# Seven-product scores, masks made ahead in layer 0, and early rows beside the signs: one change of a graph-attention kernel

## Chip, cores, metric

One core of one Trainium2 chip. The time is that of the device in microseconds (us), the median of several executions. One row of work is 128 nodes. "Before" and "after" are the two kernels. "Layer 0" is the stage between the signs and the hidden products. In the profile PE is TensorE (the matmuls), PEld its weight loads, DVE VectorE, ACT ScalarE, POOL GpSimd and SP SyncE. BF16, F32 and F32R are number formats; a product of 512 columns costs 0.227 us in F32R and 0.86 us in F32 (worked out in the prediction). "In order" means that an engine does not pass by an operation that has to wait.

## The reference

N = 4096 nodes, D = 512 features, `adj` is 4096 x 4096 in float32 and sparse.

```python
# layer 0
xw = max(sign(x), 0) @ sign(w0).T
x1 = layernorm(x + relu(adj @ xw))
# layer 1
node_att = softmax(x1 @ node_w, axis=0)
h = x1 @ edge_w
e = where(adj > 0, h @ h.T, NEG_BIG)          # the scores
edge_att = softmax(e, axis=1)
out = layernorm(x1 + (adj * (node_att * edge_att)) @ (x1 @ w1) + bias)
```

## The kernel before

It has five stages: signs, aggregation of layer 0 (32 rows), hidden products, scores, and aggregation of layer 1. A row of layer 0 reads its 128 x 4096 strip of `adj` as two transposed 1 MB halves (`at`), splits each quarter into `hi` (ScalarE) and `lo` (VectorE), and multiplies both by `xw` in F32R:

```python
# start: signs in BF16, 16 products a group of 512 nodes
nc.sync.dma_start(xt, x_t[:, ts(g, W)]...)
nc.vector.tensor_scalar(ba, xt, 0.0, None, ALU.is_gt)
...
def aggregate(b):                                # a row of layer 0
    ...
    for half in range(2):
        nc.sync.dma_start(at, adj_t[b, :, ts(half, HB), :])
        for q in range(2):
            nc.scalar.copy(hi, aq)
            nc.vector.tensor_sub(lo, aq, hi.bitcast(F32))
            for c in range(QC):
                nc.tensor.matmul(acc, hi[:, c, :], xw[:, kb, :], ...)
                nc.tensor.matmul(acc, lo[:, c, :], xw[:, kb, :], ...)
    ...                                          # VectorE: relu, layer norm
    nc.vector.tensor_tensor_reduce(scr, ...)
    nc.gpsimd.tensor_add(scr, xb, bias_b)
    nc.gpsimd.dma_start(x1_d[ts(b, P), :], scr)  # GpSimd also stores the row's other parts
```

The scores (products `pe`) are made for pairs of groups of 512 nodes, with four F32 products of K = 128 for each 128 x 512 block. VectorE makes the mask of each block there, from `adj` in F32.

## Time and profile before

2028.7 us (2028.4 to 2031.6, 4 runs). The stages below are read from the first and last start of a line's matmuls.

| Stage of before | us |
|---|---|
| start to the third row's first product (37.3 + two rows of 14.93) | 67.2 |
| from there to the first hidden product (layer 0) | 450.9 |
| hidden products | 96.4 |
| scores, to the first product of the last stage | 514.7 |
| last stage | 896.3 |

Two of the page's groups list the line, engine and operation, what it writes and reads with its shapes, then the busy time, the mean ns of one, and the idle time of the engine before it with its releaser. The third line is a transfer: its issuing queue, count, size and median us to landing.

```profile
L209 PE MATMUL acc<-xw,lo 128*128 128x512 f32 x1024 | 399.4, 390 | 0.6 <-DVE lo L205 0.5
...
L205 DVE TENSOR_TENSOR lo<-at,hi 128x1024 fp32r<-128x1024 f32 x128 | 168.7, 1318 | 147.1 <-ACT hi L203 147.1
...
at<-in_adj_t_dram SPq DMA_DIRECT2D x64, 1024.0 KB, 5.1
```

PE waited 0.6 us for `lo` in 1024 products. VectorE itself idled 147 us before `lo`, so it has slack on average.

### The profile page before, as it was taken

The numbers are of one execution on the slowest core, as the hardware profiler recorded it, in microseconds if no ns is written. First come the engines' busy times: TensorE is split into PE (matmuls) and PEld (weight loads), VectorE is DVE, ScalarE is ACT, GpSimd is POOL, SyncE is SP. The second block draws the span as 40 slices with busy tenths as digits, with TensorE's granted clock in tenths as the row PEclk, the third lists the DMA queues.
The fourth block names the chain that finished last, engine by engine and source line by source line (L and its number), as shares of the span: only waits on it lengthen the run. The fifth ranks groups of instructions, "written<-read, shape, count | busy, mean of one in ns | idle before, by whom it ended". The sixth has DMA issues, their size and how long they took to land.

```text
span 2025.5 us, 17689 instructions
## 1 busy us (share of the span) xinstructions
PE 2004.4 (99%) x6268; PEld 1108.3 (55%) x6268; DVE 1243.5 (61%) x1759; ACT 691.5 (34%) x1195; POOL 401.5 (20%) x485
## 2 busy tenths in 40 slices
PE   9999999999999999999999999999999999999997
PEld 4888888888544454545555444444444444444443
DVE  3555555556534554445545897786759775977634
ACT  4333333333113666666666521131221220222100
POOL 0243333334300000000001111140124111321101
PEclk9999999999999999999999999999999999999999
DMA  9566566565009786867767887765666765685421
GB/s 328 186 220 203 196 216 210 201 209 173 29 0 351 260 302 229 308 231 272 280 257 265 330 329 258 250 248 198 249 237 251 260 246 201 227 283 201 172 70 62
DMA packets 118153, 455.73 MB, mean 225 GB/s; under 512 B 10288, under 2 KB 10288, under 8 KB 93488
## 3 DMA queue, kind: packets, MB, share of 16 engines
q0 software_dynamic: 48128, 241.20, 31.6%
q1 hardware_dynamic: 69360, 212.36, 31.6%
q8 instruction: 49, 0.80, 0.2%
q10 hardware_dynamic: 576, 1.05, 0.1%
q14 instruction: 40, 0.33, 0.0%
HBM read 355.99 MB, written 98.57 MB: 224 GB/s over the span
## 4 chain that ended last, share of the span: by engine, by line
PE 96%; DMA 3%; DVE 1%; ACT 0%; issue 0%; SPq 0%; ACTq 0%; POOLq 0%; POOL 0%; DVEq 0%
PE ps L479 38%; PE pe L356 21%; PE acc L209 11%; PE acc L208 11%; PE po L531 5%; PE seven L89 5%; PE pt L377 3%; DMA a<-in_adj_dram 2%; PE pw L181 1%; PE pt L238 1%; DMA xt<-in_x_t_dram 1%; DVE lo L205 0%; PE ptm L405 0%; DMA xb<-x_d 0%; ACT a L342 0%
## 5 line engine op out<-in xcount | busy, mean ns | idle before, releaser
L356 PE MATMUL pe<-hT 128*128 128x512 f32 (+3 forms) x1152 | 475.5, 557 | 0.0
L479 PE MATMUL ps<-q,lop 128*128 128x512 f32 x1024 | 446.9, 592 | 0.0
L208 PE MATMUL acc<-xw,hi 128*128 128x512 f32 x1024 | 401.6, 392 | 0.0
L209 PE MATMUL acc<-xw,lo 128*128 128x512 f32 x1024 | 399.4, 390 | 0.6 <-DVE lo L205 0.5
L479 PE MATMUL ps<-t,lop 128*128 128x512 f32 x768 | 332.9, 592 | 0.0
L479 PEld LDWEIGHTS ps<-q,lop 128*128 128x128 f32 x1024 | 193.9, 190 | 240.8 <-issue 237.0
L356 PEld LDWEIGHTS pe<-hT 128*128 128x128 f32 x1152 | 205.0, 191 | 184.0 <-issue 174.8
L434 ACT ACTIVATE q<-q 128x2048 f32<-128x2048 f32 x64 | 122.3, 1911 | 407.8 <-DVE q L431 394.2
L205 DVE TENSOR_TENSOR lo<-at,hi 128x1024 fp32r<-128x1024 f32 x128 | 168.7, 1318 | 147.1 <-ACT hi L203 147.1
L479 PEld LDWEIGHTS ps<-t,lop 128*128 128x128 f32 x768 | 145.9, 190 | 183.7 <-issue 180.3
L440 DVE SCALAR_TENSOR_TENSOR q<-ac,q 128x512 f32<-128x512 f32 x256 | 198.9, 830 | 53.6 <-ACT q L434 39.1
L203 ACT CAST hi<-at 128x1024 fp32r<-128x1024 f32 x128 | 134.6, 1052 | 272.6 <-PE acc L208 271.3
L209 PEld LDWEIGHTS acc<-xw,lo 128*128 128x128 f32 x1024 | 192.3, 188 | 41.0 <-DVE lo L205 1.7
L208 PEld LDWEIGHTS acc<-xw,hi 128*128 128x128 f32 x1024 | 192.3, 188 | 39.3
L338 DVE CUSTOM_DVE_ANT_0 a<-a,pe 128x512 f32<-128x512 f32 x112 | 76.7, 687 | 206.9 <-ACT s L363 206.9
L342 ACT ACTIVATE a<-a,nmax_c 128x512 f32<-128x512 f32 x256 | 183.5, 718 | 45.8 <-DVE nmax_c L338 45.5
L483 DVE TENSOR_TENSOR over<-over,ps 128x512 f32<-128x512 f32 x168 | 113.6, 681 | 107.8 <-PE ps L479 107.7
L431 DVE CUSTOM_DVE_ANT_1 q<-q,mrow 128x2048 f32<-128x2048 f32 x64 | 148.5, 2325 | 40.3 <-DMA q<-s_d 36.2
L363 ACT COPY s<-pe 128x512 f32<-128x512 f32 (+2 forms) x144 | 77.7, 543 | 138.4 <-PE pe L356 120.3
L531 PE MATMUL po<-over 128*128 128x512 f32 x256 | 115.9, 600 | 3.7 <-DVE xb L540 3.7
L425 POOL DMA_DIRECT2D ac<-in_adj_t_dram x64 | 48.8, 763 | 325.3 <-DVE q L440 253.4
L377 PEld LDWEIGHTS pt<-ident,s 128*128 128x128 f32 x496 | 62.1, 141 | 68.7 <-issue 57.7
(107 smaller groups left out, 1553.8 us busy)
## 6 DMA issues: line engine op xcount, KB each, us to landing
at<-in_adj_t_dram SPq DMA_DIRECT2D x64, 1024.0 KB, 5.1
ac<-in_adj_t_dram POOLq DMA_DIRECT2D x64, 1024.0 KB, 6.7
a<-in_adj_dram SPq DMA_DIRECT2D x64, 1024.0 KB, 7.5
q<-s_d POOLq DMA_DIRECT2D x64, 1024.0 KB, 7.8
lop<-lop_d SPq DMA_DIRECT2D x112, 512.0 KB, 4.1
s_d<-s POOLq DMA_DIRECT2D x36, 1024.0 KB, 4.8
s_d<-t POOLq DMA_DIRECT2D x28, 1024.0 KB, 6.2
xb<-in_x_dram SPq DMA_DIRECT2D x32, 256.0 KB, 3.1
```

The lines of the kernel that those rows point to most:

```text
L203: nc.scalar.copy(hi, aq)
L205: nc.vector.tensor_sub(lo, aq, hi.bitcast(F32))
L208: nc.tensor.matmul(acc, hi[:, c, :], xw[:, kb, :], start=(kb == 0), stop=False)
L209: nc.tensor.matmul(acc, lo[:, c, :], xw[:, kb, :], start=False, stop=(kb == NB - 1))
L342: lambda: nc.scalar.activation(e, e, AF.Exp, bias=nmax_c[:, b, c : c + 1], scale=-1.0, accum_out=sum_c[:, b, c : c + 1])
L356: nc.tensor.matmul(pe[:, lo * P :], hT[:, k, ts(A * BG + i, P)], hT[:, k, (B * BG + lo) * P : (B + 1) * W], start=(k == 0), stop=(k == KD ...
L377: nc.tensor.transpose(pt[:, j, :], s[:, i, ts(j, P)], ident)
L431: nc.vector._custom_dve(TENSOR_ADD_SAT, out=q, in0=q, in1=mrow.unsqueeze(1).to_broadcast([P, BG, W]), s0=0.0, s1=-HUGE)
L434: nc.scalar.activation(q, q, AF.Exp)
L440: nc.vector.scalar_tensor_tensor(qc, a[:, :, c, :], 0.0, qc, ALU.max, ALU.mult)
L479: nc.tensor.matmul(ps, lop[:, c, ts(h, P)], rop[m][:, c, :], start=(c == 0), stop=(c == BG - 1))
L531: nc.tensor.matmul(po, (lower if k // 2 else upper)[:, k % 2, ts(i, P)], w1_s[:, k, :], start=(k == 0), stop=(k == KD - 1),)
```

## The change

It has four parts:

1. **Scores.** The blocks of two pairs of groups are multiplied together in seven products instead of eight.
2. **Masks.** Most masks are made in layer 0, in 80 pieces: a piece of `adj` is loaded (512 KB), turned into a BF16 mask in place by VectorE, and stored (256 KB). The scores load that.
3. **Light pairs last.** The cheap score pairs come at the end, beside the first loads of the last stage.
4. **Signs.** Two rows of signs ride in one F32R product. Rows 0 and 16 of layer 0 are aggregated beside the signs.

The core of the diff, with cuts and in another order:

```diff
+        pieces = deque((r, j, c) for r in range(NG) for j in range(BG) for c in range(0, r + 1, 2))
+        pair = wp.tile([P, 2, 2 * W], F32, name="pair", tag="we_s")
+        single = wp.tile([P, 2 * W], F32, name="single", tag="quarter", bufs=2)
+        bufs = deque([pair[:, 0, :], pair[:, 1, :], single])
+        def premask():
+            if loaded and (len(loaded) == 2 or not pieces):
+                (r, j, c), a = loaded.popleft()
+                m = a.bitcast(BF16).rearrange("p (c w) -> p c w", c=2)[:, :, :W]
+                nc.vector.tensor_scalar(m, a.rearrange(...), 0.0, NEG_BIG, ALU.is_le, ALU.mult)
+                nc.gpsimd.dma_start(mask_d[r][:, c : c + 2, j, :], m)
+                bufs.append(a)
+            if pieces:
+                r, j, c = pieces.popleft()
+                a = bufs.popleft()
+                nc.gpsimd.dma_start(a, adj[ts(r * BG + j, P), c * W : (c + 2) * W])
+                loaded.append(((r, j, c), a))
         def aggregate(b):
...
-            for half in range(2):
+            for half in range(0 if b in early else 2):
...
                     nc.vector.tensor_sub(lo, aq, hi.bitcast(F32))
+                    if (half, q) != (0, 0):
+                        premask()
...
+        early = [0, HB]
+        def halves(g):                       # slices of the two early rows
+            for n, b in enumerate(early):
+                nc.sync.dma_start(a, adj_t[b, :, ts(g, BG), :])
+                nc.scalar.copy(hi[:, ts(n, BG), :], a)
+                nc.vector.tensor_sub(lo[:, ts(n, BG), :], a, ...)
...
-                nc.vector.tensor_scalar(ba, xt, 0.0, None, ALU.is_gt)
+                nc.vector.tensor_scalar(over, xt[:, :, W // 2 :], 0.0, TWO, ALU.is_gt, ALU.mult)
+                nc.vector.scalar_tensor_tensor(ba, xt[:, :, : W // 2], 0.0, over, ALU.is_gt, ALU.add)
...
+    class Couple:                            # two pairs of groups, seven products
+        def quad(self, q, between):
+            multiply(y, 0, True); nc.scalar.copy(c11, y)
+            multiply(x, 1, True); nc.vector.tensor_add(c11, c11, x)
+            multiply(y, 5); nc.scalar.copy(c12, y)
+            ...
```

## The prediction

> **What bounds the kernel now.** I read the page from the top: busy time per engine, the slices, the chain that ended last; then PE's waits, the busy time of each engine by stretch, and PE's timeline for the pitch of its matmuls.
>
> From the page of the kernel before:
>
> ```profile
> PE 2004.4 (99%) x6268; PEld 1108.3 (55%) x6268; DVE 1243.5 (61%) x1759; ACT 691.5 (34%) x1195; POOL 401.5 (20%) x485
> ...
> PE 96%; DMA 3%; DVE 1%; ACT 0%; issue 0%; SPq 0%; ACTq 0%; POOLq 0%; POOL 0%; DVEq 0%
> ```
>
> PE is busy for 2004.4 of 2025.5 us and is 96% of the chain, so the time is the sum of PE's work plus 21 us of gaps. Whatever removes PE work shortens the kernel, unless a new wait comes in.
>
> Its busy time by stretch (window; length, PE, PEld, DVE, ACT, POOL busy; clock, DMA share, GB/s): the start, layer 0, the scores, the aggregation.
>
> ```profile
> 5.00:35.00 30.00, 27.17 (x121) 11.71 (x120) 13.66 (x19) 16.11 (x28) 0.00 (x0) 1.00 1.04 391
> 200.00:400.00 200.00, 200.00 (x911) 165.51 (x910) 113.14 (x147) 66.34 (x80) 68.79 (x76) 1.00 0.63 206
> 614.00:1129.00 515.00, 510.55 (x1652) 262.60 (x1651) 260.44 (x614) 328.96 (x783) 39.40 (x72) 1.00 0.76 278
> 1129.00:1984.00 855.00, 855.00 (x2018) 380.10 (x2018) 634.36 (x680) 169.88 (x163) 164.71 (x191) 1.00 0.65 233
> ```
>
> The start is limited by the transfers (391 GB/s, share 1.04); the rest by PE, with room on the others.
>
> A matmul's "mean ns" is its latency, so its price must come from start to start in the timeline (start, duration, what):
>
> ```profile
> 1082.66 3.60 PE L356 MATMUL pe<-hT 128*128 128x512 f32 x8
> 1086.10 0.60 PE L377 MATMUL pt<-ident,s 128*128 128x128 f32 x4
> 1086.53 1.02 PE L356 MATMUL pe<-hT 128*128 128x512 f32 x2
> ```
>
> Eight F32 passes take 1086.10 - 1082.66 = 3.44 us. A 512-column F32 product is two records (1152 records for 576 products), so it costs 2 x 0.43 = **0.86 us**; four transposes cost 0.43.
> - BF16: the signs' group has 128 matmuls in 28.6 us busy, about **0.22 us** each, some of it waiting at the start.
> - F32R: a row of layer 0 is 64 matmuls and 4 transposes, 68 records. 911 records in 200 us are 13.4 rows, 14.93 us each; less 0.43 that is **0.227 us** per matmul.
>
> [...] the one-source mask (128x2048, F32) takes 1.22 us, the two-source `lo` takes that for 128x1024.
>
> **The change part by part.**
>
> *Scores.* 24 of the 28 off-diagonal blocks are now done in 12 couples. A couple has 2 x 7 x 2 = 28 products in place of 32: 12 x 4 = 48 F32 products fewer. 48 x 0.86 = **-41 us**, all on PE's path. The transposes stay at 496. PE's work in the stage falls from 511 to about 470 us.
>
> The other engines there: DVE loses 45 us of masks (64 x 1.22, then 48 x 0.69), 12 of row statistics and 9 of combining that moves to the next stage; it gains 72 additions of PSUM (50 us) and 60 operand sums (48 us). 260 becomes about 292 of 470, 62%. ACT: 55 us of block copies go, 96 copies of 0.58 us (56) come, the exponentials lose 21: about 309, 66%. Neither is a bound. The accumulators are rewritten only after ACT has copied them, but products of another quadruple (1.7 to 3.4 us) mostly stand between, against a copy of 0.58. I allow **+5 us** for copies stuck behind exponentials.
>
> PE waited 4.5 us at this stage's start; the masks now come as halves of the size. **-4.5 us.**
>
> *Signs.* 128 BF16 matmuls (28.6 us) become 64 in F32R (64 x 0.227 = 14.6). In PE work that is -14 us. The first two aggregated rows (128 matmuls, 29.1 us) move beside them, to fill the gaps of the start. Before, PE reaches the third row at 37.3 + 2 x 14.93 = 67.2 us. PE alone would now need only 14.6 + 29.1 = 44 us from about 12.
>
> But the built program's order has a loop through a transfer. For each group g: SyncE issues the 1 MB load for g+3 when `ba` of g is made (its buffer), then behind it on the same queue the two adjacency slices of g (256 KB each). VectorE makes `lo` of slice g before `ba` of g+1. So one turn is:
> - 1 MB from issue to landing, 5.1 us (median of `at`), plus 0.26 MB at 391 GB/s, 0.7;
> - `hi`, 512 columns on ACT: 0.55;
> - `lo`, 512 columns with two sources: 0.69;
> - `ba`, 1024 columns with two sources: 1.22;
> [...]
>
> That is **8.4 us a turn**, where PE needs 24 x 0.227 = 5.5. The first `ba` that the loop governs (group 1) I put at 20.5 us: the four DVE steps per weight slice (1.8 us) end at 12.5, then the third 1 MB load and the first slices land at 18, then `hi`, `lo`, `ba`. Six turns later it is 71; the last slice lands at 76.5, its `hi` and `lo` are ready at 79, its matmuls end at **81**. Against 67.2 this is **+14 us**: the saved PE work is more than eaten by a latency chain.
>
> *Masks in layer 0.* 80 pieces, three per row: loads of 524 KB, a one-source DVE pass of 0.69 us, stores of 262 KB in BF16. DVE per row: 113.14 / 13.4 + 3 x 0.69 = 10.5 of 14.93 us. Transfers per row: 206 GB/s x 14.93 us = 3.08 MB, plus 2.36, makes 5.44 MB or 364 GB/s, 93% of the 391 shown. It fits, but barely; a late piece holds up DVE in order, and `lo` behind it, which has only about 1.2 us of slack (it ends 2.3 us into a quarter of 3.6). I allow **+6 us** over 27 rows.
>
> *Light pairs last.* They let the first block's scaling be prepared beside PE's last score pairs. PE had no gap there before: 0.
>
> Sum: -41 - 4.5 + 5 + 14 + 6 = -20.5; 2028.5 - 20.5 = **2008 us**, -1.0%.
>
> **The rivals.**
> 1. *The start is PE-bound after all.* If the slices land early or the loop is slacker, PE passes the third row at about 57 to 60 us, and the start gains 8 to 10 instead of losing 14: about 1985. For it: the start's transfers fall to some 190 GB/s, so their queue is nearly empty. Against it: an empty queue still takes 5 us for 1 MB.
> 2. *Layer 0 becomes bound by transfers.* If stores of 1 KB pieces and loads together reach only 340 GB/s, a row takes 5.44 / 0.34 = 16 us, +1.1 x 27 = 29: about 2031. For it: 93% of the best rate. Against it: 391 was held for 30 us, and 418 occurs in single windows of 10 us.
> 3. *Waits in the scores.* A chain PE, ACT, DVE, PE in every quadruple that costs 1 us would be 24 us, about 2027. For it: many more hand-overs between PE and ACT. Against it: interleaving of two quadruples, 62 to 66% load.
>
> **Range and chances.** With the start good and no other waits: 2028.5 - 41 - 4.5 - 9 = 1974. With two of the losses full: about 2045. Eight in ten: 1978 to 2034. Faster by 2% means below 1988, which needs rival 1 and few other waits: 0.24. Above 2069 needs all losses at once: 0.05.
>
> **What would show it.** In the profile after: the third row's first matmul near 81 us and gaps of about 3 us in PE before each `lo` of the slices (right), or 57 to 60 (rival 1). A row pitch of 14.9 to 15.2 us in layer 0, transfers near 360 GB/s (right), or 16 (rival 2). The scores from first product to first aggregation in about 475 us, against 514. The aggregation unchanged at 855 us. It would be wrong if PE waits inside the scores, or if the loop of the start runs faster than 7 us a turn.

Cut from the prediction are passages that rest on no trace or run of this case, among them a term of 0.2 us in the turn of the start. The terms left there add up to 8.3 us, where the turn was put at 8.4. That a matmul's mean is its latency shows in before: `lo` matmuls have a mean of 390 ns and follow the one before them by 0.227 us. The turn's 0.55, 0.69 and 1.22 us are estimates from operations of before (`hi` and `lo` of 1024 columns took 1.05 and 1.22 us, VectorE's additions of 512 columns 0.68); after shows 0.62, 0.69 and 1.22. That a small load behind a big one on the same queue lands after it was my assumption; e1 and f4 below test it (third row at 80.8 and 70.2 us).

## The result and the profile after

After takes **2174.7 us** (2170.7 to 2178.5, 4 runs) against 2028.7 before. It is 7.2% slower (ratio 1.0716, 95% interval 1.0694 to 1.0737). A ratio here is the mean time of one kernel's fast runs over that of the other's fast runs of the same rounds, so it is not quite the ratio of the medians quoted.

| Stage | before | after | difference | predicted |
|---|---|---|---|---|
| start to the third row | 67.2 | 86.3 | +19.1 | +14 |
| layer 0 | 450.9 | 600.1 | **+149.2** | +6 |
| hidden products | 96.4 | 96.4 | 0 | 0 |
| scores | 514.7 | 495.6 | -19.1 | -40.5 |
| last stage | 896.3 | 894.6 | -1.7 | 0 |

One stage explains the result. From the page of after, these are the busy times, the 40 slices of PE's busy tenths and of its granted clock, and the group that stood at 0.6 us before:

```profile
PE 2015.5 (93%) x6108; PEld 1119.2 (52%) x6108; DVE 1340.4 (62%) x1896; ACT 672.3 (31%) x1107; POOL 555.7 (26%) x683
...
PE   6867767779999999989999989999999999999997
...
PEclk8988988889999999999999999999999999999999
...
L295 PE MATMUL acc<-xw,lo 128*128 128x512 f32 x960 | 402.3, 419 | 101.2 <-DVE lo L289 101.1
```

The first nine slices, 489 us, show PE at six to eight tenths, with a lowered clock in most of them. PE now waits 101.1 us for `lo`. The busy times by stretch (length; PE, PEld, DVE, ACT, POOL busy with counts; clock; DMA share; GB/s) show the masks' rows and, once the pieces are used up, rows without them:

```profile
200.00:400.00 200.00, 147.83 (x565) 114.96 (x565) 93.11 (x131) 41.05 (x52) 91.54 (x123) 0.86 0.83 281
500.00:600.00 100.00, 100.00 (x455) 82.46 (x454) 57.32 (x76) 32.94 (x41) 32.99 (x38) 1.00 0.64 215
```

At 68 records a row, 565 records in 200 us are 24 us a row, against 14.95 at the end. No engine is full and the queues move **less** than planned: 281 GB/s, where three pieces a row at full pace would need 364. The waits of all engines from 100 to 490 us (waiter and releaser; us in total, times, longest) say who holds whom:

```profile
DVE pair L266 <- DMA pair<-in_adj_dram: 129.2, 43, 8.5
...
PE acc L295 <- DVE lo L289: 94.3, 29, 7.7
POOL pair L272 <- DMA mask_d<-pair: 80.1, 24, 8.9
DVE single L266 <- DMA single<-in_adj_dram: 53.6, 23, 7.3
...
POOL single L272 <- DMA mask_d<-single: 36.1, 8, 7.7
```

VectorE waits for pieces, and GpSimd waits for the stores of masks to land before it may load into the same buffer. One turn of it, in the timeline of GpSimd (start, duration, what; in brackets the idle time before it and its releaser):

```profile
241.11 0.71 POOL L267 DMA_DIRECT2D mask_d<-single  x1
241.81 0.57 POOL L272 DMA_DIRECT2D pair<-in_adj_dram  x1
242.37 0.73 POOL L267 DMA_DIRECT2D mask_d<-pair  x1
249.26 0.57 POOL L272 DMA_DIRECT2D single<-in_adj_dram  x1 [6.16 <-DMA mask_d<-single]
```

And the same moment in the timeline of all engines:

```profile
250.56 0.69 DVE L266 TENSOR_SCALAR pair<-pair 128x1024 bf16<-128x1024 f32 x1 [7.98 <-DMA pair<-in_adj_dram]
...
252.50 1.21 DVE L289 TENSOR_TENSOR lo<-at,hi 128x1024 fp32r<-128x1024 f32 x1
...
253.76 0.80 PE L295 MATMUL acc<-xw,lo 128*128 128x512 f32 x1 [4.25 <-DVE lo L289]
...
255.63 0.63 PE L295 MATMUL acc<-xw,lo 128*128 128x512 f32 x1
...
256.06 0.63 PE L294 MATMUL acc<-xw,hi 128*128 128x512 f32 x1
```

The load issued at 241.81 lands when VectorE goes on at 250.56. VectorE stood in its order for 7.98 us, and `lo` stands behind the mask, so PE stood for 4.25 us. PE then starts a matmul every 0.43 us, not every 0.23, until 258.6; the granted clock from 253.76 to 258.60 us is 0.50. From 100 to 500 us PE had 17 gaps of 3.4 to 7.7 us, and after 16 of them matmuls ran at 0.43 us for 3.1 to 6.1 us; after none of its 11 gaps of 0.5 to 1.5 us did they. In the 3 us after a gap the granted clock was 0.50 for those 16, 0.61 for the other long one and 1.00 for each of the 11.

The loss adds up. Waits for `lo` make 101.1 us. From 100 to 500 us PE was busy for 299.7 us over 1146 records, which at the full rate (14.93 us for 68) would be 251.6. The slow stretches therefore add 48.1. Together that is **149.2 us**, the whole of layer 0's loss (that it fits to the decimal is chance).

So far this names the waits, not their cause. Theories: (1) the built order bunches the pieces, with four to six in some rows and VectorE's `lo` behind them; (2) **B**, the round of a buffer (load, mask, store, next load), with GpSimd held in its order until a store lands, is too long for three buffers; (3) **C**, the bytes are too many. (The expectations of the first batch use letters of their own; what held is said under each.)

### The profile page after: what moved, and what is told of

Read it like the earlier page. It is cut to its first block, busy times and chain, and to the rows that moved or that the text cites. A ratio compares the mean times of both kernels' runs of the same rounds, so it can differ in the third digit from the quotient of the medians.

```text
span 2173.0 us, 18035 instructions
## 1 busy us (share of the span) xinstructions
PE 2015.5 (93%) x6108; PEld 1119.2 (52%) x6108; DVE 1340.4 (62%) x1896; ACT 672.3 (31%) x1107; POOL 555.7 (26%) x683
## 3 DMA queue, kind: packets, MB, share of 16 engines
q10 hardware_dynamic: 576, 1.05, 0.1%
## 4 chain that ended last, share of the span: by engine, by line
PE 46%; DMA 4%; issue 3%; DVE 2%; POOL 0%; ACT 0%; POOLq 0%; DVEq 0%
PE ps L828 35%; PE seven L642 5%; PE po L881 4%; DMA s_d<-slot 1%; DMA lent<-in_adj_dram 1%; DVE line L505 1%; DMA s_d<-lent 1%; PE pt L543 1%; DMA lent<-in_adj_t_dram 0%; DMA slot<-in_adj_t_dram 0%; DVE lent L505 0%; DMA xb<-x_d 0%; ACT line L514 0%; DVE lent L504 0%; POOL s_d L659 0%
## 5 line engine op out<-in xcount | busy, mean ns | idle before, releaser
L295 PE MATMUL acc<-xw,lo 128*128 128x512 f32 x960 | 402.3, 419 | 101.2 <-DVE lo L289 101.1
L828 PE MATMUL ps<-lent,lop 128*128 128x512 f32 x992 | 432.6, 592 | 0.0
L828 PE MATMUL ps<-slot,lop 128*128 128x512 f32 x800 | 351.9, 594 | 0.0
L828 PEld LDWEIGHTS ps<-lent,lop 128*128 128x128 f32 x992 | 188.3, 190 | 236.3 <-issue 231.3
L828 PEld LDWEIGHTS ps<-slot,lop 128*128 128x128 f32 x800 | 152.2, 191 | 190.1 <-issue 185.4
L573 PE MATMUL pe<-hT 128*128 128x512 f32 (+3 forms) x384 | 134.7, 493 | 0.0
L514 ACT ACTIVATE line<-line,nmax_c 128x512 f32<-128x512 f32 x160 | 114.9, 724 | 58.8 <-DVE nmax_c L505 58.6
L742 DVE CUSTOM_DVE_ANT_1 slot<-slot,line 128x2048 f32<-128x2048 f32 x31 | 73.0, 2356 | 49.1 <-DMA slot<-s_d 49.1
L505 DVE CUSTOM_DVE_ANT_0 line<-lent,slot 128x512 f32<-128x512 bf16 x144 | 92.0, 686 | 15.2 <-ACT slot L544 9.5
L742 DVE CUSTOM_DVE_ANT_1 lent<-lent,line 128x2048 f32<-128x2048 f32 x33 | 83.0, 2519 | 25.9 <-DMA lent<-s_d 24.7
L642 PE MATMUL seven<-hT 128*128 128x512 f32 x192 | 89.7, 594 | 0.0
```

Source lines behind the costliest of these rows:

```text
L295: nc.tensor.matmul(acc, lo[:, c, :], xw[:, kb, :], start=False, stop=(kb == NB - 1))
L505: nc.vector.tensor_tensor_reduce(line, mask, src, -1.0, HUGE, ALU.add, ALU.min, accum_out=nmax_c[:, b, c : c + 1])
L514: nc.scalar.activation(line, line, AF.Exp, bias=nmax_c[:, b, c : c + 1], scale=-1.0, accum_out=sum_c[:, b, c : c + 1])
L573: nc.tensor.matmul(pe[:, lo * P :], hT[:, k, ts(A * BG + i, P)], hT[:, k, (B * BG + lo) * P : (B + 1) * W], start=(k == 0), stop=(k == KD ...
L642: nc.tensor.matmul(ps, left[m][:, k, q, :], right[m][:, k, :], start=(first and k == 0), stop=(k == KD // 2 - 1), skip_group_check=not first,)
L742: nc.vector._custom_dve(TENSOR_ADD_SAT, out=q, in0=q, in1=mrow.unsqueeze(1).to_broadcast([P, BG, W]), s0=0.0, s1=-HUGE)
```

## The experiments

15 kernels ran, in six batches, each batch with before on the same chip. Where a kernel's masks are wrong it is said so. The `adj` values and their place in the last stage stay right, and all of them still passed the comparison with the reference. One must not conclude from "correct" that a mask was right. In each batch before took 2026.5 to 2027.6 us.

| Run | us | ratio to before | third row | layer 0 | scores |
|---|---|---|---|---|---|
| after | 2174.7 | 1.072 | 86.3 | 600.1 | 495.6 |
| e1_no_masks | 2022.7 | 0.998 | 80.8 | 454.3 | 493.0 |
| e2_three_per_row | 2163.6 | 1.067 | 81.3 | 589.0 | 494.0 |
| e3_masks_on_gpsimd | 2278.2 | 1.124 | 80.4 | 708.0 | 494.6 |
| e5_slices_own_queue | 2155.4 | 1.063 | 73.8 | 594.8 | 493.3 |
| f1_store_from_own_buffers | 2141.3 | 1.056 | 80.4 | 577.0 | 494.5 |
| f6_traffic_alone | 2117.7 | 1.045 | 82.1 | 552.1 | 492.2 |
| f3_no_stores | 2020.6 | 0.997 | 81.2 | 452.6 | 492.7 |
| f4_no_masks_own_queue | 2015.5 | 0.994 | 70.2 | 454.3 | 496.4 |
| f7_lead_and_spare_buffers | 2062.0 | 1.017 | 85.3 | 492.6 | 494.2 |
| f9_bytes_at_the_pace | 2022.3 | 0.997 | 81.6 | 452.5 | 493.9 |
| f10_store_a_turn_later | 2030.0 | 1.001 | 73.6 | 462.3 | 495.7 |
| g1_start_of_before | 2016.6 | 0.995 | 72.0 | 456.1 | 495.4 |
| g2_later_pieces | 2017.5 | 0.995 | 73.7 | 458.1 | 494.5 |
| g3_early_steps_later | 2019.5 | 0.996 | 73.2 | 458.5 | 497.1 |
| g4_pieces_tied_to_rows | **2009.7** | 0.992 | 67.0 | 453.2 | 496.7 |

(The three columns on the right are us of the profiled run. For the four g kernels and before, "third row" is the first row's first product plus 29.9. The expectations of e1 and f1 quote layer 0 up to a line of hidden products that starts some 3 us later: 603.5 us for after, 592 for e2.)

### First batch: which part, and is it the order?

**e1_no_masks** leaves the pieces out. The scores read one block of zeros (wrong masks).

```diff
-                    if (half, q) != (0, 0):
-                        premask()
-                nc.sync.dma_start(self.mask, mask_d[r][:, c])
+                nc.sync.dma_start(self.mask, zero_d)
```

> The changed kernel without the mask pieces of layer 0 (no loads, no VectorE masking, no stores); the scores read one block of zeros in the same amount and shape instead, so the result is wrong on purpose and the score stage moves the same bytes. Layer 0 took 603.5 us from the third row to the first hT product against 454.3 before. Theory A (the pieces alone cause it): this falls back to 448 to 456 us (30 rows of 14.95) and the whole kernel to 2020 to 2030. Rival B (the loss comes from elsewhere in the new start, from the lowered clock or the early rows' accumulators held in PSUM): it stays above 500 us. Start unchanged at 86 us, scores at about 495 us under both.

Layer 0 falls to 454.3 us and the time to 2022.7. The total fits theory A of its expectation; layer 0, 457.7 us by the expectation's measure, is just over the 456 allowed. So the masks in layer 0 cost about 150 us. All other parts together gain 5 us, which is not clear of noise (ratio 0.9977, interval 0.9948 to 1.0006).

**e2_three_per_row** holds each piece behind the `lo` that it stands at in the program. The built order then has exactly three pieces a row.

```diff
-                    nc.vector.tensor_sub(lo, aq, hi.bitcast(F32))
+                    made = nc.vector.tensor_sub(lo, aq, hi.bitcast(F32))
                     if (half, q) != (0, 0):
-                        premask()
+                        with tc.issue_after(made.ins):
+                            premask()
```

> Order only: each masking instruction may stand on VectorE no earlier than behind the lo of the quarter it was written after, so the built order has 3 pieces per row where the changed kernel has 4 to 6. Bytes, buffers and instructions are the same. Theory A1 (too many pieces per row for a cycle of load, mask, store through three buffers, about 14 us, 4.7 us per piece): 3 pieces need 14.1 us of a row's 14.95, so the row pitch falls to 15 to 16.5 us, layer 0 to 455 to 500 us, total 2030 to 2075. Rival A2 (bytes: 5.4 MB per row at the 339 GB/s per full share that the profile after shows): pitch 16 us, total near 2060. Rival A3 (the order does not matter, only the latency of each piece): still 80 pieces at 5 us, layer 0 near 600.

Layer 0 goes from 600.1 to 589.0 us, 11 us of 149. The order is **not** the cause; the waits only spread over more rows. Of its three theories only A3, that the order does not matter, comes near. Its busy times in the stretch of 200 to 400 us:

```profile
200.00:400.00 200.00, 167.86 (x708) 134.16 (x707) 117.05 (x142) 51.16 (x62) 91.23 (x120) 0.91 0.79 276
```

Its largest waits from 100 to 500 us, those of ScalarE left out:

```profile
POOL single L272 <- DMA mask_d<-single: 114.1, 19, 8.1
POOL pair L272 <- DMA mask_d<-pair: 96.7, 30, 6.7
DVE pair L266 <- DMA pair<-in_adj_dram: 87.6, 18, 9.8
```

The 708 records are 10.4 rows, 19.2 us a row. GpSimd stands 211 us in its order for stores to land.

**e3_masks_on_gpsimd** makes the masks on GpSimd instead of VectorE (`nc.gpsimd.tensor_scalar`), to take the waiting for pieces off VectorE.

> The masking instruction moves from VectorE to GpSimd; same bytes, same three buffers, correct result. VectorE then never waits for a piece, so lo and PE no longer stand behind one. Theory A (head-of-line wait on VectorE): PE's wait for lo in layer 0 falls from 101 us to under 25, row pitch 15 to 16 us, total 2025 to 2060. Rival B (transfers are the limit): the pitch stays over 18 us because the row's own 2 MB come late. [...]

It is the slowest of all, 2278.2 us, where 2025 to 2060 were expected. The mask takes GpSimd 3.70 us (mean from 100 to 500 us), against 0.69 on VectorE when nothing disturbs it (0.80 on average for `pair` in after). VectorE still waits, now for GpSimd's store of the row itself, which stands behind the masks. The largest such wait from 100 to 500 us:

```profile
DVE scr L299 <- DMA x_d<-scr: 172.1, 15, 18.4
```

So the run does not test VectorE's waits for pieces alone, as it was meant to: it put over three more us a piece on GpSimd, and what stands in order behind them came late. Whether VectorE's own passes cost anything is left to f3.

**e5_slices_own_queue** issues the slices of the early rows from GpSimd's queue, so that no 1 MB load stands ahead of them on SyncE's.

```diff
-                nc.sync.dma_start(a, adj_t[b, :, ts(g, BG), :])
+                nc.gpsimd.dma_start(a, adj_t[b, :, ts(g, BG), :])
```

> The adjacency slices of the two early rows are issued on GpSimd's queue, so they no longer queue behind the 1 MB load of the signs. Layer 0 and scores as in the changed kernel. Theory (the start is a loop through the transfer, 8.3 us a turn measured): a turn falls to 5.5 to 6.5 us and the third row starts at 62 to 72 us in place of 86; total lower by 15 to 24. Rival (VectorE's and ACT's own work, or the order of operations, sets the turn): over 7.5 us a turn, third row after 80 us.

The third row starts at 73.8 us in place of 86.3, just outside the range expected. Against e2's 81.3, another build with the slices on SyncE's queue, it is 7.5 us earlier. The total is 19 us lower than after, within the 15 to 24 expected. The queue order at the start costs time, as the prediction's loop says, but this is a small part of the loss.

### Second batch: round of buffers or bytes?

**f1_store_from_own_buffers** has the order of e2. The mask goes to two small buffers that take the place of the third piece buffer.

```diff
-        bufs = deque([pair[:, 0, :], pair[:, 1, :], single])
+        bufs = deque([pair[:, 0, :], pair[:, 1, :]])
+        outs = single.bitcast(BF16).rearrange("p (n c w) -> p n c w", n=2, c=2)
-                m = a.bitcast(BF16).rearrange(...)[:, :, :W]
+                m = outs[:, out_n[0] % 2]
```

> The three pieces a row of e2_three_per_row, but the mask is written into one of two small buffers of its own (together as large as the third piece buffer, which goes), so a piece buffer is free for the next load as soon as VectorE has read it, and not when the store has landed. Bytes, instructions and their order are those of e2_three_per_row (2163.6 us, layer 0 592 us from the third row to the hidden products, 19.5 us a row). Theory B (a buffer's round of load, mask, store and GpSimd's waits in order takes 19.5 us, so three buffers pass three pieces in it): the store leaves the round, row 15.0 to 16.5 us, layer 0 460 to 500, total 2030 to 2075. Theory C (the bytes, 4.9 MB a row, are what the queues can't carry beside the rows): row and total unchanged within 20 us, 2145 to 2180.

It gained 22 us, far from the 90 or more that B expected. It misses because the edit took something away too: with two piece buffers a load can't be issued before the mask just ahead of it is made. That leaves two turns (7.5 us at the shortest) for a load that took 7.9 us to land. From 100 to 500 us:

```profile
POOL mask_d L270 <- DVE single L269: 123.5, 29, 9.0
DVE single L269 <- DMA pair<-in_adj_dram: 120.2, 18, 11.8
```

**f6_traffic_alone** loads and stores all pieces, but nothing reads them (wrong masks).

> Wrong masks on purpose (the scores read zeros). The loads and the stores of all 80 pieces are issued at three a row, the same bytes as e2_three_per_row, but nothing on VectorE reads a loaded piece and no store waits for a mask: traffic without the round of buffers. Theory C (bytes): layer 0 stays near 590 us, total 2130 to 2170. Theory B (the round and VectorE's waits in order): layer 0 460 to 480 us as without masks, total 2023 to 2045.

It is inconclusive by my own mistake. With nothing to wait for, GpSimd ran ahead of the rows: 47 pieces in 200 us, not 40. It then stood 150 us for buffers to be overwritten, with the row's own stores behind them, so VectorE waited for those (waits from 100 to 500 us):

```profile
POOL pair L275 <- DMA pair<-in_adj_dram: 150.1, 47, 10.0
...
DVE scr L303 <- DMA x_d<-scr: 89.4, 14, 11.9
```

That is traffic **and** a blocked queue. It can't speak for the bytes.

**f3_no_stores** keeps loads and masks of e2 and leaves the stores out (zeros in the scores, wrong masks).

```diff
-                nc.gpsimd.dma_start(mask_d[r][:, c : c + 2, j, :], m)
```

> Wrong masks on purpose (the scores read zeros). As e2_three_per_row, loads and masks kept, stores left out: the round of a buffer is load, mask, next load, and the bytes of a row fall by 0.75 MB. Theory B: the piece no longer waits for 5.5 us of store, three buffers pass three pieces in under 15 us: layer 0 460 to 500 us, total 2025 to 2070. Theory C: the bytes fall by 15 per cent of 4.9 MB, so layer 0 falls to about 505 to 530, total 2070 to 2100.

Layer 0 is 452.6 us, as if there were no masks at all. That is better than the 460 to 500 of theory B. 80 loads and 80 VectorE passes are free, even with three buffers. Busy times from 200 to 400 us:

```profile
200.00:400.00 200.00, 200.00 (x910) 165.60 (x909) 150.23 (x186) 67.22 (x81) 97.85 (x119) 1.00 0.85 308
```

So the stores make the loss. That holds under B (their landing in the round) and, less well, under C (C expected 505 us or more).

**f4_no_masks_own_queue** is e1 with e5's edit.

> Wrong masks on purpose (the scores read zeros). No masks in layer 0 as e1_no_masks (2022.7 us), and the slices of the two early rows issued from GpSimd's queue as e5_slices_own_queue: is the start's gain kept when nothing else is in the way? If the start gains what e5_slices_own_queue showed (12.5 us to the third row): 2006 to 2014. If the time comes back in layer 0: 2018 to 2024.

It took 2015.5 us, between its two ranges, with the third row at 70.2. Against e1 (80.8) only the queue of the slices differs. Even with its own queue and without masks, the changed start is 3 us later than that of before.

### Third batch: the same bytes, without the waits

**f7_lead_and_spare_buffers** (right masks) issues the next load ahead of the mask and its store, and writes the first 64 masks into eight buffers of their own. The room for these is in the transposed rows, split into one tile per group, of which two stay empty until row 24.

```diff
+        spare = [x1T[g].bitcast(BF16)[:, k, :]... for g in (HG - 1, NG - 1) for k in range(KD)]
         def premask():
+            if pieces:
+                a = bufs.popleft()
+                nc.gpsimd.dma_start(a, adj[...])
+                loaded.append(((r, j, c), a))
+            if len(loaded) == 3 or (loaded and not pieces):
+                (r, j, c), a = loaded.popleft()
+                m = spare[made_n[0] % 8] if made_n[0] < 64 else a.bitcast(BF16)...
                 nc.vector.tensor_scalar(m, a..., 0.0, NEG_BIG, ALU.is_le, ALU.mult)
                 nc.gpsimd.dma_start(mask_d[r][:, c : c + 2, j, :], m)
```

> Right masks. Three pieces a row as e2_three_per_row (2163.6 us), the same bytes and the same VectorE work, but the first 64 masks are written into eight buffers of their own (columns of the transposed rows that only the last rows fill), and the next load stands ahead of the mask and its store on GpSimd's queue. So loads run as far ahead as in f3_no_stores (where they cost nothing, 2020.6 us), and no wait for a store's landing is left. Theory B (the round of a buffer through its store, with GpSimd held in order): layer 0 460 to 480 us for those pieces, total 2025 to 2060. Theory C (the bytes: f3's 308 GB/s plus 50 GB/s of stores are more than the queues carry beside the rows): layer 0 over 550 us, total 2110 to 2170.

The kernel falls from 2163.6 to 2062.0 us with every byte kept, at a **higher** rate (346 GB/s, against 276 in e2). Layer 0 is 96 us shorter; B had expected 109 to 129, and a total up to 2060. What is left shows in the waits from 100 to 450 us:

```profile
POOL mask_d L275 <- DVE rstd L152: 118.8, 22, 8.9
...
DVE x1T L274 <- DMA pair<-in_adj_dram: 24.9, 15, 5.4
```

GpSimd now stands waiting for the mask just being made, and the next load stands behind it. (The releaser named is VectorE's operation next to the mask.)

**f9_bytes_at_the_pace** is what f6 should have been. Each transfer is tied to VectorE's place in the row by a write of one column, with buffers as in f7, and no mask is made (wrong masks). 64 of the 80 stores are issued.

```diff
+                nc.vector.memset(a[:, :1], 0.0)
                 nc.gpsimd.dma_start(a, adj[...])
...
-                nc.vector.tensor_scalar(m, ...)
-                nc.gpsimd.dma_start(mask_d[r][:, c : c + 2, j, :], m)
+                if made_n[0] <= 64:
+                    nc.vector.memset(m[:, :, :1], 0.0)
+                    nc.gpsimd.dma_start(mask_d[r][:, c : c + 2, j, :], m)
```

> Wrong masks on purpose (the scores read zeros). f6_traffic_alone was not paced: nothing tied its transfers to the rows, and it issued 47 pieces in 200 us where 40 were meant. Here every load and store is tied to VectorE's place in the row by a write of one column [...], with three buffers for the loads and eight for the stores; no mask is made and VectorE never waits for a load just issued. Traffic of 64 pieces at three a row, without the waits. Theory C: PE busy in 100 to 400 us falls to 75 to 85 per cent, total 2110 to 2160. Theory B: PE stays at 98 to 100 per cent, total 2020 to 2045.

Theory C falls. From 200 to 400 us:

```profile
200.00:400.00 200.00, 200.00 (x911) 165.52 (x910) 116.24 (x224) 67.38 (x81) 122.61 (x159) 1.00 0.97 361
```

The queues carry 361 GB/s at a share of 0.97, and PE loses nothing in 200 us. Landings are longer (9.6 us for a piece in `pair`, 9.9 for a store), but nobody stands waiting for one just issued.

### Fourth batch: the cause removed, and the start undone

**f10_store_a_turn_later** (right masks) issues a mask's store one turn after the mask, gives the last masks three buffers of their own, and takes e5's queue.

```diff
+            if masked:
+                (r, j, c), m = masked.popleft()
+                nc.gpsimd.dma_start(mask_d[r][:, c : c + 2, j, :], m)
             if len(loaded) == 3 or (loaded and not pieces):
...
-                nc.gpsimd.dma_start(mask_d[r][:, c : c + 2, j, :], m)
+                masked.append((piece, m))
```

> Right masks, meant to beat both kernels. As f7_lead_and_spare_buffers (2062.0 us), and the store of a mask is issued one turn after the mask, so GpSimd no longer stands in its queue waiting for the mask just being made (118.8 us of such waits in f7) and the next load is not held behind it; the last masks get three buffers of their own, and the slices of the early rows go to GpSimd's queue (f4_no_masks_own_queue: third row at 70.2 us). If GpSimd's place in order was the rest of the cause, layer 0 falls to 452 to 458 us, as in f9_bytes_at_the_pace, with PE at 98 to 100 per cent: total 2012 to 2022. If something else is left (VectorE's 10 us a row of work beside landings of 8 to 10 us), layer 0 stays over 475 us, total 2035 to 2060.

While the eight buffers serve, layer 0 runs at full pace **with** right masks. Its busy times from 200 to 400 us:

```profile
200.00:400.00 200.00, 200.00 (x910) 165.54 (x909) 148.43 (x187) 66.71 (x81) 122.12 (x160) 1.00 0.95 364
```

A wait of VectorE that is left later, among the three last buffers:

```profile
DVE late L279 <- DMA mask_d<-late: 13.7, 9, 3.3
```

Against after, layer 0 has lost 138 of its 149 us of excess. With f3 (no stores, no loss) and f9 (the bytes, no loss) this shows B: a store's landing, and GpSimd's in-order wait for it, in the round of three buffers. The runs don't split these two. Standing in order is no loss by itself: GpSimd still stood 108.0 us here from 100 to 500 us, now at the next load until VectorE had read its buffer (the releaser named is again the operation next to the mask), and PE was busy for 396.7 of those 400 us. The total missed its range, though: 2030.0 us in place of 2012 to 2022. In the profiled run the third row comes at 73.6, not 70.2 (e5, which also loads pieces, had 73.8), and layer 0 is 8 us over the 454 without masks. The other executions were 5 us slower than the profiled one, and nothing here says why.

**g1_start_of_before** has the same masks with the start of before (signs in BF16, no early rows).

> Right masks. The same masks as f10_store_a_turn_later with the start of the kernel before: signs in BF16 and no early rows. It undoes that one part. Third row's first product at 67 us as before, against 70.2 with the changed start on its own queue and 86.3 in the changed kernel. If the changed start costs and gains as those figures say, this kernel is 2 to 5 us faster than f10_store_a_turn_later: 2007 to 2018. If the changed start gains something later that its third row doesn't show, f10_store_a_turn_later is faster. Against the kernel before only the scores' seven products and the masks remain as changes: by the scores of e1_no_masks (20 us shorter) 2008 expected.

At 2016.6 us (ratio 0.9953, interval 0.9936 to 0.9970) it is faster than before by under 1%, clear of noise, and faster than f10 by 13 us. The total is in the range expected, but the gain over f10 was to be 2 to 5, so the direction holds and the size doesn't. The signs and early rows are a loss here, not a gain. Of the 8.4 us between the two profiled runs only 1.6 lie before the third row and 6.2 in layer 0; why there is not shown. But its first row began at 42.1 us, where before has 37.3.

### Fifth and sixth batch: what was left

**g2_later_pieces** starts the pieces in row 1, slows them to 2.5 a row from row 22 on, and uses the eight buffers for 63 masks.

```diff
-                    if (half, q) != (0, 0):
+                    if n and (half, q) != (0, 0) and (n < 22 or n % 2 == 0 or q):
```

> Right masks. As g1_start_of_before (2016.6 us), but no piece is loaded in row 0, so that the start's own loads are alone on the queues; from row 22 on 2.5 pieces a row in place of 3; and 63 masks, not 56, use the eight buffers. If the pieces' loads held up the start, the first row begins at 37.3 us as before, not at 42.1; if the three late buffers cost the 5 us in layer 0, it takes 481 us from the first row's first product to the hidden products, not 486. Both: 2005 to 2010. Neither: 2014 to 2020.

A miss: the first row still begins at 43.8 us, from there to the hidden products it takes 488.0 us where 481 were hoped for, and the time is the same within the spread (2017.5). The list of transfers issued before 45 us says why: the first piece loads are still there.

```profile
pair<-in_adj_dram POOLq DMA_DIRECT2D x2, 512.0 KB, 7.9
single<-in_adj_dram POOLq DMA_DIRECT2D x1, 512.0 KB, 10.0
```

Their place in the program is no wait. GpSimd has nothing before them, so they go out at the start.

**g3_early_steps_later** lets the first early steps of the last stage wait ten turns for their loads, not five (`self.since[n] + 10`).

> As g2_later_pieces, and the first aggregation's early steps wait ten turns, not five, after the issue of their loads before VectorE works on them, in the last part of the scores. If VectorE's wait in order for that load makes the waits of TensorE at the end of the scores (7 us of 20), these go and the scores are 4 to 8 us shorter than in g2_later_pieces. If the waits come from the copies and buffers of the scores themselves, the scores stay within 2 us; the early steps may then also end later and cost the aggregation some us.

A miss: the scores take 497.1 us, not less than g2's 494.5. It does not remove PE's waits there, so my reading of their cause is not shown.

**g4_pieces_tied_to_rows** is g2 with one column of each of the first three buffers written by VectorE in its row, so their loads can't leave earlier.

```diff
+                if not made_n[0]:
+                    nc.vector.memset(a[:, :1], 0.0)
                 nc.gpsimd.dma_start(a, adj[...])
```

> Right masks. As g2_later_pieces (2017.5 us), and VectorE writes one column of each of the first three piece buffers at its place in row 1, so that their loads can't be issued before it. If the three loads held up the start, the first row's first product comes at 37 to 38 us, not 43.8, and the total is 2010 to 2013. If not, it stays near 43 us and 2015 to 2019.

The first row comes where the signs of before put it (timeline of PE):

```profile
37.14 0.58 PE L252 MATMUL acc<-xw,hi 128*128 128x512 f32 x1
```

The time is **2009.7 us**, ratio 0.9918 (0.9901 to 0.9935), the best of all. It is 0.8% under before: clear of noise, but small. It keeps the seven products and the masks in layer 0, and pays 2.3 us for 80 pieces there (453.2 against 450.9).

## Why the prediction was wrong, by its own steps

**What bounds the kernel.** PE bound it before (96% of the chain that ended last). The prediction's own rule, "unless a new wait comes in", is what happened.

**The step that failed is "Masks in layer 0", the term +6 us.** It measured +149. The step counted VectorE's busy time (10.5 of 14.93 us) and bytes (93% of 391 GB/s) and concluded "It fits, but barely". Both counts were near (f10 at full pace: 148.43 us of VectorE over 13.4 rows, 11.1 a row, and 364 GB/s) and neither was the question: f9 carries those bytes and f10 those bytes and passes at full pace. It even named the danger ("a late piece holds up DVE in order, and `lo` behind it"), but gave it a size by feel. What it did not work out is the round of a buffer. Three buffers must pass three pieces in 14.95 us. A piece's load took 5.0 to 6.7 us to land in after (medians by buffer), its mask 0.7 and its store 4.9 to 5.3, and between these stand the turns of two in-order engines. In e2 the row took 19.2 us. There the medians without any standing add up to 11.3 us for `pair` (5.1 + 0.7 + 5.5) and 12.5 for `single` (4.8 + 0.7 + 7.0), from 100 to 500 us; these sums are estimates. So only 2 to 4 us of queueing were free, and one late landing, such as the 8.7 us of the load shown above, or GpSimd's 6.16 us for a store, used them up.

The trace of e2 shows the wait: GpSimd stood 211 us at loads that waited for a store's landing, with what came behind them in its order. I had reckoned with an order of that kind on the start's queue and did not apply the thought to GpSimd.

**Rival 2**, layer 0 bound by transfers, guessed the right stage with the wrong mechanism and a fifth of the size (+29). f9 refutes the mechanism.

**The clock** as a cost of waiting was not in the prediction at all. After a wait such as the 4.25 us shown, matmuls ran at half pace for 3 to 6 us (0.43 us each, granted clock 0.50). That added 48 us to the 101 of waits.

**Signs and early rows, +14.** The loop through the load was right: the turn measured 8.3 us (`ba` started at 44.8, 53.1 and 61.4 in after), predicted 8.4 (its terms add up to 8.5, 8.3 without the one that is cut). In e1, without masks, the third row started at 80.8, predicted 81. After itself shows 86.3. Builds with the same signs on SyncE's queue spread from 80.4 to 86.3, and what makes those 5 us was not tried apart. The queue order is shown by e1 against f4: 80.8 to 70.2 with nothing else changed. Even so the start came later than the 67.0 of g4, which has the start of before, so the change is a loss there.

**Scores, -40.5.** Measured: -19.1. The busy times by stretch over the scores of before:

```profile
614.95:1129.20 514.25, 509.80 (x1652) 262.42 (x1651) 260.53 (x615) 329.16 (x783) 39.40 (x72) 1.00 0.76 278
```

And of after:

```profile
783.30:1278.40 495.10, 475.36 (x1562) 245.75 (x1561) 304.11 (x641) 311.07 (x693) 70.13 (x112) 0.99 0.71 253
```

The 48 products did go (960 records of 512 columns became 864), but busy time fell by 34.4 us, not 41; why the rest is missing was not traced. VectorE (304 us) and ScalarE (311) came near the forecast of 292 and 309. PE's waits there grew from 4.5 to 19.7 us, where I had +5 for copies and -4.5 for the start. Of these, 7.6 stand in three waits at the end (PE's waits of after):

```profile
PE pt L543 <- ACT lent L583: 7.6, 3, 3.4
```

That is where the light pairs run, which I had put at 0. The chain read in the trace (VectorE waits 6.7 us for a block of the last stage, ScalarE and then PE behind it) did not stand the test of g3, so its cause stays open. **Rival 3** (some 24 us of waits in the scores) was nearer in size than my main line, but not in its place: of the 19.7 us only 7.4 stand at the products of the quadruples (`seven`).

**Aggregation.** Predicted unchanged, measured -1.7 us: right.

**The BF16 price** of 0.22 us held some waiting at the start. The trace of before has 16 products of the signs in 3.63 us with 0.38 of latency, 0.217 each.

## What to carry to other kernels

Hidden work on a second path passes at most as many pieces as it has buffers in one round of a buffer: add up load, pass, store and each in-order turn between them, and compare it with the pace of the path it hides behind; bytes and busy time don't show it (f9 carried 361 GB/s without a loss, e2 lost at 276). Write results to buffers of their own, issue loads ahead of stores that must still wait, and issue such a store a turn late. Here the first two took layer 0 from 589.0 us to 492.6 (f7), the third, with three more buffers and another queue at the start, to 462.3 (f10), and g4, with the start of before and a slower pace in the last rows, to 453.2, without removing a byte. And a place in the program is no wait: three piece loads that depended on nothing were issued before 45 us in g2, and once they were tied to the rows in g4 the first row came at 37.14 us in place of 43.8.
